# Block ends of a two-layer graph network on one core: transposes by part of the identity in two steps, quotients between two adds, the output's last part in two

## The chip, the cores and the metric

One Trainium2 chip, one NeuronCore. The metric is the device time of one execution in microseconds (us); times shown are medians of several runs. The profile is of one further execution.

## The reference

A graph with 3327 nodes of 128 features and a 0/1 adjacency matrix goes through two layers. Layer 0 is a mean aggregation with batch normalisation; layer 1 is attention in which the adjacency matrix is added (twice) to the scores. `q`, `k` and `v` are reshaped as (128, 3327, 8), so there are 128 attention problems, here called batches, with head size 8. Cut to what matters:

```python
h = relu(layernorm(x))
agg = adj.T @ h / deg
y = agg @ W_n.T + b_n + h @ W_c.T + b_c
x = x + relu(batchnorm(y))                       # layer 0
h = relu(layernorm(x))
q, k, v = ((h @ W.T).reshape(128, n, 8) for W in (Wq, Wk, Wv))
a = einsum('dnh,dmh->dnm', q, k) * 128**-0.5 + adj + adj
out = einsum('dnm,dmh->dnh', softmax(a, axis=2), v)
x = x + out.reshape(n, 1024) @ Wo.T              # layer 1
```

## The kernel before

The order of instructions on each engine is the order in which the program writes them; no scheduler moves them, and semaphores are set from the tiles that instructions share.

**Layer 0** takes some 250 us. At its end the new `x` (`xs`, 26 chunks of 128 rows) is stored to the DRAM tensor `xd` by `keep_nodes`: the first two quarters of four chunks from `residual`, the other 18 chunks at the end on SP's DMA queue. The normalised, transposed activations are stored to `hd` by `keep_columns` on POOL's queue. Then POOL and ACT copy the first set of keys into place, and attention starts.

**Attention** works in `NG` = 32 groups of four batches. A group goes through seven query blocks of 476 columns (`QB`; the last has 472), a block through `SU` = 13 steps, 2912 steps in all. The keys lie in 26 chunks of 128; a step handles four pairs of (key chunk, half of the batches). For each pair `product` (L742) makes the scores of two batches, 128 x 952, in one of three pairs of PSUM banks (`psc`). There are two ways from scores to weights:

- *Plain pairs*: VectorE adds the adjacency to the scores (`add`, L852), and one ACT exponential per step (`late`, L895, issued a step later) handles the two or three plain tiles `d`.
- *Weighted pairs*: ACT takes the exponential of the raw scores (`weighted`, L861), and POOL multiplies it by an exponential of the adjacency read from the DRAM tensor `wd` (L864).

Ten steps have three plain pairs and one weighted; the steps in `DOUBLE` = (3, 7, 11) have two of each. Three steps later (`LAG`) `second(0)` and `second(1)` multiply the weights with `v` (`weigh`, L618) and sum over the chunks in PSUM tile `av`: nine rows for each of four batches, at partitions 0, 32, 64 and 96; the ninth row is the sum of weights. `av` has two buffers, used in turn by the blocks.

**A block's end** is the generator `finish`, driven one part at a time by `step()` in the steps of `PARTS`, at the end of the step between its last product and `second(1)`. With the lag these are steps of the next block. Before, the parts are: at step 3 the copy of `av` to `avs` (L628); at step 5 four transposes of it (L633), each of every fourth column (`J` = 4, so 119 columns, or 118 after the last block), against the whole identity; at step 7 the quotients (L640 to L643: clip, reciprocal, product) on VectorE; at step 8 the store of the result to `att`.

**Side work** uses the `av` bank that a block's end has just left free. `begin`, called after `second(1)`, starts a part at step 7 or 11 (`DOUBLE[1:]`), `go_on` carries it on. In blocks 0 to 2 of a group these are the six halves of the projections of later rows (`projection`, L208, then a VectorE copy `pf` or `ov`, L214 to L236, and stores); in blocks 3 and 4 the output of the rows before (`outputs`): two sets of four transposes (`turn`, L269), then `last`, eight accumulated matmuls with `Wo` (L277) and the addition of `xj` (L282), with the store to `out`.

In group 0 the weights `wd` of the first query columns are there, and `more_weights` makes those of each next block: it loads two chunks of the adjacency (`t`, SP's queue), takes their exponential on ACT (L770), and stores them to `wd`, one pair of chunks in each three steps. Also in group 0, `others` holds 16 loads of the first group's `q` beyond column 512; SP issues two in each step from step 0. SP's queue also carries the fetches of adjacency (`at`, L730) and weights (`wt`, L726), two steps ahead (`PRE`).

The lines around the change in a step:

```python
add(0, product(i, y, *plain[0]))
second(0)
add(1, product(i, y, *plain[1]))
if len(rest) > 1:
    weighted(rest[1][0], product(i, y, *rest[1]))
else:
    add(2, product(i, y, *plain[2]))
if s in PARTS:
    step()
if s - 1 in DOUBLE and x + 1 < len(steps):
    coming = first(x + 1)
second(1)
begin(i, y, s)
go_on(i, y, s)
```

Of the kernel before, what the change touches and what calls it, by code (L numbers as in the profile page):

```python
# [9 lines left out]
F32 = mybir.dt.float32  # L10
# [9 lines left out]
D = 128  # L20
H = 8
P = 128
NC = 26
T = N * D
NP = NC * P
NB = 512
QB = 476
G = 4
# [4 lines left out]
WC = 18  # L33
CH = 4 * NP // D
NG = D // G
DOUBLE = (3, 7, 11)
PARTS = (3, 5, 7, 8)

def pieces(r):

    return [(p0, p1) for p0, p1 in ((0, r // 16 * 16), (r // 16 * 16, r)) if p1 > p0]
# [3 lines left out]
def tile_two_layer_gnn(  # L47
# [17 lines left out]
    nc = tc.nc  # L65
# [6 lines left out]
    qblocks = [(n0, min(QB, NP - n0)) for n0 in range(0, NP, QB)]  # L72
# [16 lines left out]
    wd = dram.tile([NC - WC, P, NP], F32, name="wd")  # L89
    xd = dram.tile([NP, D], F32, name="xd")  # L90
# [163 lines left out]
    def outputs(wk, j):  # L254

        r = min(CH, N - j * CH)
        t = wk.tile([P, H, D], F32, name="t4")
        nc.sync.dma_start(
            t[:CH].rearrange("p e j -> p (e j)"), atr[j * CH : (j + 1) * CH, :]
        )  # L260
        xj = wk.tile([P, D], F32, name="xj")
        nc.sync.dma_start(xj[:CH], xd[j * CH : (j + 1) * CH, :])
        tT = wk.tile([P, H, P], F32, name="t4")

        def turn(e):
            bank = yield
            pt = bank.rearrange("p (i q) -> p i q", i=4)
            for i in range(4):
                nc.tensor.transpose(pt[:, i, :CH], t[:CH, 4 * e + i, :], ident[:CH, :CH])  # L269
            yield  # L270
            nc.vector.tensor_copy(tT[:, 4 * e : 4 * e + 4, :CH], pt[:, :, :CH])
            yield

        def last():
            bank = yield
            for e in range(H):
                nc.tensor.matmul(  # L277
                    bank[:CH, :D], tT[:, e, :CH], wo[:, e, :], start=(e == 0), stop=(e == H - 1)
                )
            yield  # L280
            y = wk.tile([P, D], F32, name="y")
            nc.vector.tensor_add(y[:CH], bank[:CH, :D], xj[:CH])  # L282
            yield
            for p0, p1 in pieces(r):
                nc.sync.dma_start(out[j * CH + p0 : j * CH + p1, :], y[p0:p1])

        return [turn(0), turn(1), last()]

    def drive(part, bank=None):

# [7 lines left out]
    with tc.tile_pool(name="l0", bufs=1) as l0, tc.tile_pool(  # L298
        name="l0adj", bufs=3
# [42 lines left out]
        def stats(i, root=True):  # L342
            cs = range(4 * i, min(NC, 4 * i + 4))
            for c in cs:
                nc.vector.bn_stats(st[:, c, :], xs[:, c, :])
            for c in cs:
                nc.vector.bn_aggr(mv[:, c, :], st[:, c, :])
            if root:
                roots(4 * i, min(NC, 4 * i + 4))

        def roots(c0, c1):
            nc.scalar.activation(sd[:, c0:c1], mv[:, c0:c1, 1], AF.Sqrt, bias=eps)
# [176 lines left out]
        def keep_nodes(cs):  # L529
            nc.sync.dma_start(  # L530
                xd.rearrange("(c p) d -> p c d", p=P)[:, cs, :], xs[:, cs, :]
            )

        def residual(i):
            pt, cs = turned(i, A, acc[i])
            nc.vector.tensor_add(xs[:, cs, :], xs[:, cs, :], pt)
            if i < 2:
                keep_nodes(cs)

        def second_norm(i, engine):  # L540
# [14 lines left out]
        def keep_columns(i0, i1):  # L555
            s = slice(4 * i0 * P, min(NC, 4 * i1) * P)
            nc.gpsimd.dma_start(hd[:, s], B2[:, s])
# [37 lines left out]
        for i in range(2, NQ):  # L595
            if i > 2:
                residual(i)
            stats(i, False)
        roots(4, NC)
        factors(4, NC)  # L600
        for i in range(1, NQ):
            second_norm(i, nc.gpsimd if i % 3 == 0 else nc.vector)
        for i in range(1, NQ):
            columns(i, i % 2 == 0)
        keep_nodes(slice(8, NC))
        keep_columns(0, NQ)
        for x, c in enumerate(range(0, NC, 4)):
            n = min(4, NC - c)
            (nc.scalar.copy if x % 2 else nc.gpsimd.tensor_copy)(
                k[:, c : c + n, :],  # L610
                ks.bitcast(F32).rearrange("g (p c) -> g c p", c=NC)[:, c : c + n, :],
            )

# [7 lines left out]
    def finish(rp, av, d0, n0, w):  # L623

        J = 4
        R = -(-w // J)
        avs = rp.tile([P, QB], F32, name="avs")
        nc.vector.tensor_copy(avs[:, : R * J], av[:, : R * J])  # L628
        yield

        pt = av.rearrange("p (j q) -> p j q", j=J)
        for j in range(J):
            nc.tensor.transpose(  # L633
                pt[:R, j, :], avs[:, j : j + (R - 1) * J + 1 : J], ident
            )
        yield
        pv = pt.rearrange("p j (b h) -> p b j h", h=32)
        ri = rp.tile([P, G, J], F32, name="ri")

        nc.vector.tensor_scalar(ri[:R], pv[:R, :, :, H], 1e-30, None, ALU.max)  # L640
        nc.vector.reciprocal(ri[:R], ri[:R])  # L641
        o = rp.tile([P, G, J, H], F32, name="oq")
        nc.vector.tensor_tensor(  # L643
            o[:R], pv[:R, :, :, :H], ri[:R].unsqueeze(3).to_broadcast([R, G, J, H]),
            ALU.mult,
        )
        yield

        r, j = divmod(min(w, N - n0), J)
        nc.sync.dma_start(  # L650
            attb[bass.ds(d0, G), n0 : n0 + r * J, :].rearrange(
                "b (p j) h -> p b (j h)", j=J
            ),
            o[:r].rearrange("p b j h -> p b (j h)"),
        )
        if j:
            nc.sync.dma_start(
                attb[bass.ds(d0, G), n0 + r * J : n0 + r * J + j, :].rearrange(
                    "b (o j) h -> o b (j h)", o=1
                ),  # L660
                o[r : r + 1, :, :j, :].rearrange("p b j h -> p b (j h)"),
            )
# [4 lines left out]
    def attention():  # L667


        with tc.tile_pool(name="adj", bufs=4) as ap, tc.tile_pool(  # L670
# [13 lines left out]
            if True:  # L684
# [69 lines left out]

                def more_weights(i, y, s):

                    k, phase = s // 3, s % 3
                    if i or y + 1 >= len(qblocks) or k > 3:
                        return
                    n0, w = qblocks[y + 1]  # L760
                    c = WC + 2 * k
                    n = min(2, NC - c)
                    if phase == 0:
                        have["w"] = wk.tile([P, 2, QB], F32, name="t4")
                        nc.sync.dma_start(
                            have["w"][:, :n, :w], adjr[:, c : c + n, n0 : n0 + w]
                        )
                    elif phase == 1:
                        a = have["w"][:, :n, :w]
                        nc.scalar.activation(a, a, AF.Exp, bias=low, scale=2.0)  # L770
                    else:
                        nc.sync.dma_start(
                            wd[c - WC : c - WC + n, :, n0 : n0 + w].rearrange("c p n -> p c n"),
                            have["w"][:, :n, :w],
                        )

# [51 lines left out]
                for x, (i, y, s) in enumerate(steps):  # L830
# [7 lines left out]
                    while pending and (total - len(pending)) * (SU * len(qblocks) - FROM[i] - 4) <= k * total:  # L838
                        pending.pop(0)()
                    more_weights(i, y, s)  # L840
                    for args in others[:2]:
                        nc.sync.dma_start(*args)
                    del others[:2]
                    due = len(waiting) == LAG
                    plain, rest = pairs(s)
                    d = ep.tile([P, 3, 2, QB], F32, name="d")
# [2 lines left out]
                    def add(j, p):  # L849
                        c = plain[j][0]  # L850

                        nc.vector.scalar_tensor_tensor(  # L852
                            d[:, j, :, :w],
                            have[0, i, y, c // 2][:, c % 2, :w]
                            .unsqueeze(1).to_broadcast([P, 2, w]),
                            SAFE / 2, p[:, :, :w], ALU.min, ALU.add,
                        )
# [18 lines left out]
                        late()  # L876
                    add(0, product(i, y, *plain[0]))
                    second(0)
                    add(1, product(i, y, *plain[1]))
                    if len(rest) > 1:  # L880
                        weighted(rest[1][0], product(i, y, *rest[1]))
                    else:
                        add(2, product(i, y, *plain[2]))
                    if s in PARTS:
                        step()

                    if s - 1 in DOUBLE and x + 1 < len(steps):
# [15 lines left out]
                    step()  # L903
                while ending:
                    step()
                for p, b in zip(outputs(wk, NG - 1), (0, 1, 0)):
                    drive(p, avs2[b])
                    drive(p)
                    drive(p)
# [73 lines left out]
    def general():  # L983
# [65 lines left out]
        with tc.tile_pool(name="gw2", bufs=2) as wk, tc.tile_pool(  # L1049
            name="gp2", bufs=1, space=PSUM  # L1050
        ) as gp:
            banks = [gp.tile([P, NB], F32, name=f"h{i}") for i in range(3)]
            for j in range(NG):
                for p, b in zip(outputs(wk, j), banks):
                    drive(p, b)
                    drive(p)
                    drive(p)
# [47 lines left out]
```

## Time and profile before

| | us |
|---|---|
| median of 3 runs | 10390.24 |
| lowest, highest | 10385.12, 10391.82 |
| profiled execution, its own time | 10385.98 |
| its span, first to last instruction | 10384.2 |
| busy: TensorE (PE) | 9816.7 |
| busy: weight loads (PEld, beside PE) | 2888.6 |
| busy: VectorE (DVE) | 9331.0 |
| busy: ScalarE (ACT) | 9925.5 |
| busy: GpSimd (POOL) | 8443.5 |

Busy times overlap, so they are compared with the span one by one. Matmuls are pipelined, and the ends that the profile gives them are modelled; a busy PE is not a PE at its peak. A group row gives line, engine, operation, output<-inputs, shapes and count, then busy us and the mean ns of one, then the idle time before them and what ended it. A row of the timeline gives start and duration in us and, in brackets, the engine's idle time just before and who ended it. `PEld s L742 <- DVE d L852` in the waits means that the weight load of line 742 had to wait for the VectorE instruction of line 852.

### The profile page before, as it was taken

How to read it: one execution, taken by the hardware profiler on the slowest of the kernel's cores; microseconds unless marked ns; L12 is line 12 of the kernel's file. 1: busy time of each engine (PE TensorE's matmuls, PEld its weight loads, DVE VectorE, ACT ScalarE, POOL GpSimd, SP SyncE). 2: the span in 40 equal slices, each digit the busy share in tenths (PEclk: the TensorE clock that was granted, in tenths of full speed). 3: DMA queues.
4: the chain of work that ended last, by engine and by line, in shares of the span. 5: the costliest groups of instructions: out<-in, count | busy, mean ns of one | idle time of the engine just before them, and what ended most of it. 6: DMA issues, size and time to landing. Idle time of an engine off the chain costs nothing.

```text
span 10384.2 us, 188013 instructions
## 1 busy us (share of the span) xinstructions
PE 9816.7 (95%) x72431; PEld 2888.6 (28%) x72431; DVE 9331.0 (90%) x9501; ACT 9925.5 (96%) x6655; POOL 8443.5 (81%) x4316
## 2 busy tenths in 40 slices
PE   7899999999999999999999999999999999999998
PEld 3222222222222222222222222222222222222222
DVE  5689999999999999999999999999999999999998
ACT  4789999999999999999999999999999999999998
POOL 1678888888888888888888888888888888888887
PEclk9899999999999999999999999999999999999999
DMA  6765666665666665666655666655666555666554
GB/s 232 205 178 161 164 168 167 168 165 158 168 167 168 167 162 161 168 169 168 167 159 163 168 169 167 164 165 159 171 168 167 162 164 164 169 168 165 159 153 129
DMA packets 1115994, 1735.87 MB, mean 167 GB/s; under 512 B 194606, under 2 KB 1091756, under 8 KB 1107404
## 3 DMA queue, kind: packets, MB, share of 16 engines
q1 hardware_dynamic: 1110558, 1717.86, 60.2%
q8 instruction: 568, 9.31, 0.4%
q10 hardware_dynamic: 4350, 4.20, 0.1%
q14 instruction: 342, 2.80, 0.1%
q0 software_dynamic: 176, 1.71, 0.0%
HBM read 1621.05 MB, written 102.38 MB: 166 GB/s over the span
## 4 chain that ended last, share of the span: by engine, by line
POOL 21%; PE 16%; ACT 8%; issue 5%; DVE 3%; DMA 0%; POOLq 0%; ACTq 0%; SPq 0%; DVEq 0%
POOL f L864 20%; PE av L618 8%; PE s L742 6%; ACT f L861 5%; ACT d L895 3%; DVE d L852 2%; PE av L633 1%; POOL k L192 1%; PE av L208 1%; PE av L277 0%; POOL o L238 0%; POOL o L237 0%; DVE oq L643 0%; DVE ri L641 0%; DVE avs L628 0%
## 5 line engine op out<-in xcount | busy, mean ns | idle before, releaser
L864 POOL TENSOR_TENSOR f<-f,wt 128x952 f32<-128x952 f32 (+1 forms) x3584 | 7944.8, 2235 | 1680.6 <-ACT f L861 1660.7
L852 DVE SCALAR_TENSOR_TENSOR d<-at,s 128x952 f32<-128x952 f32 x8064 | 8754.4, 1140 | 606.2 <-PE s L742 447.7
L895 ACT ACTIVATE d<-d 128x2856 f32<-128x2856 f32 (+1 forms) x2912 | 7055.5, 2423 | 12.5 <-DVE d L852 2.3
L618 PE MATMUL av<-d,v 128*9 128x476 f32 x32256 | 5072.3, 567 | 1.9 <-ACT d L895 1.9
L742 PE MATMUL s<-q,k 32*128 32x476 f32 x23296 | 4108.3, 476 | 407.9 <-ACT f L861 334.1
L861 ACT ACTIVATE f<-s 128x952 f32<-128x952 f32 (+1 forms) x3584 | 3436.4, 980 | 224.7 <-PE s L742 220.9
L742 PEld LDWEIGHTS s<-q,k 32*128 32x128 f32 x23296 | 1772.8, 182 | 5631.8 <-DVE d L852 3296.9
L618 PE MATMUL av<-f,v 128*9 128x476 f32 x14336 | 2853.4, 566 | 0.0
L618 PEld LDWEIGHTS av<-d,v 128*9 128x9 f32 x32256 | 583.6, 88 | 1162.3 <-issue 1131.8
L618 PEld LDWEIGHTS av<-f,v 128*9 128x9 f32 x14336 | 316.6, 88 | 153.1 <-issue 139.6
L192 POOL CAST k<-ks 128x256 fp32r<-128x256 f32 x434 | 284.6, 656 | 0.0
L633 PE MATMUL av<-ident,avs 128*119 128x128 f32 (+1 forms) x896 | 241.3, 392 | 0.8 <-DVE avs L628 0.8
L633 PEld LDWEIGHTS av<-ident,avs 128*119 128x119 f32 (+1 forms) x896 | 198.2, 292 | 52.7 <-issue 51.1
L430 PE MATMUL acc<-a,A 128*128 128x512 f32 (+1 forms) x364 | 151.8, 570 | 23.2 <-ACT A L364 23.1
L238 POOL TENSOR_TENSOR o<-pf,o 104x512 fp32r<-104x512 f32 x124 | 159.9, 1289 | 9.9
L628 DVE COPY avs<-av 128x476 f32<-128x476 f32 (+1 forms) x224 | 144.6, 645 | 4.5 <-PE av L618 4.5
L437 DVE TENSOR_REDUCE amax<-a 128x1 f32<-128x3327 f32 x26 | 93.7, 3611 | 35.3 <-DMA a<-in_adj 35.3
L236 DVE TENSOR_SCALAR pf<-av,low_half 104x512 f32<-104x512 f32 x62 | 46.6, 751 | 72.0 <-PE av L208 70.3
L234 DVE COPY pf<-av 104x512 f32<-104x512 f32 x62 | 42.9, 692 | 73.0 <-PE av L208 71.8
L214 DVE COPY ov<-av 104x512 f32<-104x512 f32 x62 | 42.9, 692 | 67.8 <-PE av L208 67.8
L430 PEld LDWEIGHTS acc<-a,A 128*128 128x128 f32 x364 | 69.0, 192 | 108.3 <-issue 84.7
L770 ACT ACTIVATE t<-t,low_half 128x952 f32<-128x952 f32 (+1 forms) x24 | 26.2, 1090 | 65.4 <-DMA t<-in_adjT 65.4
(121 smaller groups left out, 1022.6 us busy)
## 6 DMA issues: line engine op xcount, KB each, us to landing
at<-in_adjT SPq DMA_DIRECT2D x1728, 476.0 KB
wt<-wd SPq DMA_DIRECT2D x1536, 238.0 KB
at<-in_adjT SPq DMA_DIRECT2D x288, 472.0 KB
wt<-wd SPq DMA_DIRECT2D x256, 236.0 KB
ks<-kT SPq DMA_DIRECT2D x496, 104.0 KB
q<-qT SPq DMA_DIRECT2D x496, 104.0 KB
a<-in_adj SPq DMA_DIRECT2D x26, 1663.5 KB
kT<-o SPq DMA_DIRECT2D x128, 208.0 KB
```

The source lines that it names most:

```text
L192: nc.gpsimd.tensor_copy(k[:, c : c + n, half * 64 : half * 64 + 64], ks.bitcast(F32).rearrange("g (p c) -> g c p", c=NC)[:, c : c + n, :],)
L208: nc.tensor.matmul(bank[:CH], hj, wqk[s][:, e * NB : (e + 1) * NB], start=True, stop=True)
L238: nc.gpsimd.tensor_tensor(o[:CH, 1], f[:CH], o[:CH, 0].bitcast(F32), ALU.subtract)
L430: nc.tensor.matmul(acc[i][:, :w], A[:, c, :], a[:, n0 : n0 + w], start=(c == 0), stop=(c == NC - 1),)
L618: nc.tensor.matmul(av[32 * b : 32 * b + H + 1, :w], tiles[2][:, b, c, :], e, start=first, stop=last,)
L628: nc.vector.tensor_copy(avs[:, : R * J], av[:, : R * J])
L633: nc.tensor.transpose(pt[:R, j, :], avs[:, j : j + (R - 1) * J + 1 : J], ident)
L742: nc.tensor.matmul(p[:, x, :we], k[rs, c, :], q[rs, n0 : n0 + we], start=True, stop=True,)
L852: nc.vector.scalar_tensor_tensor(d[:, j, :, :w], have[0, i, y, c // 2][:, c % 2, :w] .unsqueeze(1).to_broadcast([P, 2, w]), SAFE / 2, p[:, ...
L861: nc.scalar.activation(f[:, :, :w], p[:, :, :w], AF.Exp, scale=2.0)
L864: nc.gpsimd.tensor_tensor(f[:, :, :w], f[:, :, :w], have[1, i, y, c][:, :w].unsqueeze(1).to_broadcast([P, 2, w]), ALU.mult,)
L895: nc.scalar.activation(flat, flat, AF.Exp, scale=2.0)
```

## The change

A block's end gets one part more, at step 6: the four transposes become plain matmuls of `avs` with 36 columns of the identity (nine for each batch), two at step 5 and two at step 6, and the results lie densely in the bank. At step 7 `step()` moves from after the step's last product to between its first and second plain add. `last` is split into two parts of four matmuls, the second adding to the sum of the first, so the output has four parts of side work. In layer 0 the third quarter of `xs` is stored from `residual` too, the other 14 chunks on POOL's queue ahead of the second normalisation, and the store to `hd` comes after the copies of the keys. In group 0 `more_weights` takes the exponential two steps after the load, and the store comes three after it, just ahead of the next load; the loads in `others` start at step 2. The path `general`, which this input does not take, gets a fourth bank.

```diff
-PARTS = (3, 5, 7, 8)
+PARTS = (3, 5, 6, 7, 8)
...
-        def last():
+        y = wk.tile([P, D], F32, name="y")
+
+        def last(i):
             bank = yield
-            for e in range(H):
+            for e in range(4 * i, 4 * i + 4):
                 nc.tensor.matmul(
-                    bank[:CH, :D], tT[:, e, :CH], wo[:, e, :], start=(e == 0), stop=(e == H - 1)
+                    bank[:CH, :D], tT[:, e, :CH], wo[:, e, :],
+                    start=(e == 4 * i), stop=(e == 4 * i + 3),
                 )
             yield
-            y = wk.tile([P, D], F32, name="y")
-            nc.vector.tensor_add(y[:CH], bank[:CH, :D], xj[:CH])
+            nc.vector.tensor_add(y[:CH], bank[:CH, :D], y[:CH] if i else xj[:CH])
             yield
-            for p0, p1 in pieces(r):
-                nc.sync.dma_start(out[j * CH + p0 : j * CH + p1, :], y[p0:p1])
+            if i:
+                for p0, p1 in pieces(r):
+                    nc.sync.dma_start(out[j * CH + p0 : j * CH + p1, :], y[p0:p1])
...
-        return [turn(0), turn(1), last()]
+        return [turn(0), turn(1), last(0), last(1)]
...
-            if i < 2:
+            if i < 3:
                 keep_nodes(cs)
...
+        nc.gpsimd.dma_start(
+            xd.rearrange("(c p) d -> p c d", p=P)[:, 12:, :], xs[:, 12:, :]
+        )
         roots(4, NC)
...
-        keep_nodes(slice(8, NC))
-        keep_columns(0, NQ)
         for x, c in enumerate(range(0, NC, 4)):
...
+        keep_columns(0, NQ)
...
-        pt = av.rearrange("p (j q) -> p j q", j=J)
+        pt = av[:, : J * G * (H + 1)].rearrange("p (j q) -> p j q", j=J)
+        some = ident.rearrange("p (b h) -> p b h", h=32)[:, :, : H + 1]
         for j in range(J):
-            nc.tensor.transpose(
-                pt[:R, j, :], avs[:, j : j + (R - 1) * J + 1 : J], ident
-            )
-        yield
+            nc.tensor.matmul(
+                pt[:R, j, :], avs[:, j : j + (R - 1) * J + 1 : J], some, start=True, stop=True
+            )
+            if j % 2:
+                yield
...
-                    k, phase = s // 3, s % 3
-                    if i or y + 1 >= len(qblocks) or k > 3:
+                    k, phase = divmod(s, 3)
+                    if i or y + 1 >= len(qblocks):
                         return
...
+                    if phase == 0 and k:
+                        nc.sync.dma_start(
+                            wd[c - 2 - WC : c - WC, :, n0 : n0 + w].rearrange("c p n -> p c n"),
+                            have["w"][:, :, :w],
+                        )
+                    if c == NC:
+                        return
...
-                    elif phase == 1:
-                        a = have["w"][:, :n, :w]
+                    elif phase == 2:
+                        a = have["w"][:, :, :w]
                         nc.scalar.activation(a, a, AF.Exp, bias=low, scale=2.0)
-                    else:
-                        nc.sync.dma_start(
...
-                    for args in others[:2]:
-                        nc.sync.dma_start(*args)
-                    del others[:2]
+                    if x > 1:
+                        for args in others[:2]:
+                            nc.sync.dma_start(*args)
+                        del others[:2]
...
                     second(0)
+                    if s == DOUBLE[1]:
+                        step()
                     add(1, product(i, y, *plain[1]))
...
-                    if s in PARTS:
+                    if s in PARTS and s != DOUBLE[1]:
                         step()
```

More of the change, by code (lines that the diff above doesn't have):

```diff
@@ L629, in finish @@
         yield
-        pt = av.rearrange("p (j q) -> p j q", j=J)
+        pt = av[:, : J * G * (H + 1)].rearrange("p (j q) -> p j q", j=J)
+        some = ident.rearrange("p (b h) -> p b h", h=32)[:, :, : H + 1]
         for j in range(J):
-            nc.tensor.transpose(
-                pt[:R, j, :], avs[:, j : j + (R - 1) * J + 1 : J], ident
-            )
-        yield
-        pv = pt.rearrange("p j (b h) -> p b j h", h=32)
+            nc.tensor.matmul(
+                pt[:R, j, :], avs[:, j : j + (R - 1) * J + 1 : J], some, start=True, stop=True
+            )
+            if j % 2:
+                yield
+        pv = pt.rearrange("p j (b h) -> p b j h", h=H + 1)
         ri = rp.tile([P, G, J], F32, name="ri")
@@ L761, in more_weights @@
                     c = WC + 2 * k
-                    n = min(2, NC - c)
+                    if phase == 0 and k:
[5 more added lines that the diff above has]
+                        return
                     if phase == 0:
@@ L765, in more_weights @@
                         nc.sync.dma_start(
-                            have["w"][:, :n, :w], adjr[:, c : c + n, n0 : n0 + w]
+                            have["w"][:, :, :w], adjr[:, c : c + 2, n0 : n0 + w]
                         )
-                    elif phase == 1:
-                        a = have["w"][:, :n, :w]
+                    elif phase == 2:
+                        a = have["w"][:, :, :w]
                         nc.scalar.activation(a, a, AF.Exp, bias=low, scale=2.0)
-                    else:
-                        nc.sync.dma_start(
-                            wd[c - WC : c - WC + n, :, n0 : n0 + w].rearrange("c p n -> p c n"),
-                            have["w"][:, :n, :w],
-                        )
                 extra, begun = [], []
@@ L905, in attention @@
                     step()
-                for p, b in zip(outputs(wk, NG - 1), (0, 1, 0)):
+                for p, b in zip(outputs(wk, NG - 1), (0, 1, 0, 1)):
                     drive(p, avs2[b])
@@ L1051, in general @@
         ) as gp:
-            banks = [gp.tile([P, NB], F32, name=f"h{i}") for i in range(3)]
+            banks = [gp.tile([P, NB], F32, name=f"h{i}") for i in range(4)]
             for j in range(NG):
```

## The prediction

> **What bounds the kernel now.** I read the page first, then busy times by block, then the waits, then the timeline around one block's end, then the groups kept apart by shape. The page's first line:
>
> ```profile
> PE 9816.7 (95%) x72431; PEld 2888.6 (28%) x72431; DVE 9331.0 (90%) x9501; ACT 9925.5 (96%) x6655; POOL 8443.5 (81%) x4316
> ```
>
> ScalarE (ACT) is the fullest. The stretches between block ends show which blocks leave it idle. Below are five of the seven of group 15: from the end of its second block on, each row is start:end, length, then busy time of PE, PEld, DVE, ACT, POOL.
>
> ```profile
> 5104.37:5149.28 44.91, 43.51 (x322) 12.36 (x322) 41.43 (x43) 43.78 (x30) 39.47 (x22) 1.00 0.66 185
> ...
> 5194.16:5238.49 44.33, 42.49 (x326) 12.62 (x326) 41.41 (x44) 43.65 (x30) 36.44 (x19) 1.00 0.60 160
> 5238.49:5284.05 45.56, 43.60 (x332) 13.97 (x332) 40.62 (x42) 43.56 (x30) 35.98 (x18) 1.00 0.59 159
> 5284.05:5328.16 44.11, 41.39 (x320) 11.98 (x316) 40.39 (x42) 43.44 (x30) 37.85 (x21) 1.00 0.60 149
> 5328.16:5372.24 44.08, 41.35 (x320) 11.89 (x316) 40.27 (x41) 43.38 (x30) 36.38 (x19) 1.00 0.52 156
> ```
>
> ACT's busy time is nearly constant (43.4 to 43.8), the length is not. A block with no side work takes 44.1; one with two projection halves 44.9; one with the output's `last` 45.56. The step itself is ACT's: in the timeline its `d` exponentials start 3.32 us apart in a plain step and 4.16 in a double one, without a gap. So only what makes ACT idle counts. Waits by who waited for whom:
>
> ```profile
> PEld av L208 <- DVE oq L643: 134.0, 92, 1.5
> ...
> ACT t L770 <- DMA t<-in_adjT: 65.4, 13, 10.1
> ...
> PEld av L269 <- DVE oq L643: 45.2, 31, 1.5
> ```
>
> ACT waits outright for the loads of more_weights; TensorE waits for the quotients with side work in hand. Third, the end of a block in the timeline (start, duration):
>
> ```profile
> 5021.15 0.19 PEld L742 LDWEIGHTS s<-q,k 32*128 32x128 f32 x4 [0.79 <-DVE d L852]
> ...
> 5021.57 0.94 PEld L633 LDWEIGHTS av<-ident,avs 128*119 128x119 f32 x4 [0.23 <-issue]
> ...
> 5022.64 0.10 PEld L618 LDWEIGHTS av<-d,v 128*9 128x9 f32 x3
> ...
> 5024.12 0.96 ACT L861 ACTIVATE f<-s 128x944 f32<-128x944 f32 x1 [0.70 <-PE s L742]
> ```
>
> The four transposes hold TensorE 1.07 us (5021.57 to 5022.64), and ACT's next `f` finds no scores for 0.70. So this place forgives 0.37. Why: of three score banks the step's last product takes the one that `f` frees; from there product, transposes, four weighted products and the next first product run in series while ACT does one `d`. The block with 118 columns agrees: transposes 0.64, idle 0.27. In block length the price is a little more than the idle, since an `f` that follows idle time loses its overlap with the `d` before: the step with 1.07 is 0.84 longer, that with 0.64 is 0.52.
>
> **What the Trainium skill says.** "TensorE: Matmul & The Clock Gate", section LDWEIGHTS (loading the stationary operand): a load costs its columns / 1.2 ns, whatever the depth. The weight loads by shape:
>
> ```profile
> L618 PEld LDWEIGHTS av<-d,v 128*9 128x9 f32 x32256 | 583.6, 88 | 1162.3 <-issue 1131.8 <-ACT d L895 3.7 <-ACT t L770 0.2
> ...
> L633 PEld LDWEIGHTS av<-ident,avs 128*119 128x119 f32 x768 | 181.5, 309 | 44.0 <-issue 44.0
> ...
> L277 PEld LDWEIGHTS av<-wo,t 128*104 128x104 f32 x512 | 58.3, 173 | 45.6 <-DVE oq L643 45.3 <-DVE t L271 0.3
> ...
> L633 PEld LDWEIGHTS av<-ident,avs 128*118 128x118 f32 x128 | 16.7, 195 | 8.7 <-issue 7.1 <-DVE avs L628 1.6
> ```
>
> Nine to 104 columns: (173 - 88) / 95 = 0.9 ns a column, which agrees. The transposes with 119 don't: (309 - 88) / 110 = 2.0. "FP8 and Floating Point Precision", TensorE Precision Notes: true FP32 is four passes; the trace agrees, each fp32 matmul stands as two instructions (46,592 at L618 for eight calls in each of 2,912 steps), a transpose as one. "SBUF — State Buffer", Specifications (TRN2): full bandwidth wants two hits in each 16-byte line. The slices of avs step four floats, 16 bytes, so each column is a new line. Whether that slows a plain fp32 load no instruction before shows; it is the large unknown.
>
> **The change, part by part.** Sums are made against the profiled execution, 10,386.0 us (span 10,384.2), 4 below the median 10,390.2.
>
> *1. Quotients between two adds (step 7).* Before, they sit behind step 7's last add (5029.60 to 5030.37, 0.79 with gaps), and TensorE's side work, next in its queue, waits: its load stands 1.47 after the last against 0.80 unhindered, 0.67 lost. A projection half then holds TensorE 1.04 (L208 at 5119.09, products at 5120.12), and ACT idles 0.35. For `last`, 1.92 and 1.24. Both give the same forgiveness, 0.67 + 1.04 - 0.35 = 1.36 and 0.67 + 1.92 - 1.24 = 1.35: more than before, since a double step has a second `f` here. Now the quotients start some 1.1 earlier, ahead of TensorE's need; 1.04 alone is under 1.35, as step 11 shows, where the same 1.04 meets no quotients and costs nothing. Prices by block: 0.7 three times (projections), 0.14 (output transposes), 1.55 (`last`), 3.8 a group. I leave 0.7, as DVE's copy `pf` (0.75) still stands between adds there: 3.1 x 31 groups = **96 us saved**, `last` in two included. The halves of `last` are 8 instructions, 1.05, at steps 7 and 11. It adds 32 adds of 0.29 on DVE (9 us in all, in blocks where DVE is busy 40.6 of 45.6); without that cover, +9.
> The price of the move: the second add of step 7 comes 0.79 later. Behind it stand the next step's first add and, through the bank it frees, TensorE's second product of step 8. The add after those starts at 5032.26, after 0.73 of waiting for a product, so the delay ends there; `d` of step 7 starts at 5032.40, two us after its add would now end. Nothing, or at worst 0.79 x 224 = 177.
>
> *2. The transposes.* Four transposes of one instruction become four matmuls of two, with 36 columns moving for 128, half of them at step 5, half at step 6. A half is four weight loads of 119. At 0.86 ns a column, 0.10 each, plus 0.13 for the last matmul and turnaround (the tail of the output's last, 0.31, less 0.10 for the load and 0.08 for 92 columns fewer): 0.53. Over 0.37 it leaves 0.16 idle; with the lost overlap 0.36. Fourteen halves a group cost 5.0, where now six blocks at 0.84 and one at 0.52 cost 5.5: 0.5 x 32 = **17 us saved**. Bounds: if a half fits, all 178 goes; if a load keeps the 2.0 ns of this tile (0.22 each), a half is 1.01, costs 0.78 (0.23 less than its length, as 1.07 costs 0.84), 10.9 a group: +173. I take the plain rate because nine odd columns load at it, and since L633's matmuls with 119 are slower than those with 118 too (408 ns against 300 in the same view), though their moving operand is the same: the oddness of the transpose slows both, without the step in memory.
>
> *3. more_weights.* Load, exponential one step later, store two later; now the exponential two later and the store three. ACT takes its instructions in order, so a late load holds it. The 13 waits are 10.1, 1.3, 4.0, 5.6, 5.8, 5.7, 0.8, 3.8, 5.5, 6.0, 6.3, 7.9 and 2.6; a plain step of 3.3 off each leaves 27.7: **38 saved**. The 24 exponentials stay (1.09 each). SP's store waits for the exponential, and behind it the pair's next load and the fetches; the exponential precedes the `f` whose POOL product already paces SP. Bounds 20 to 55.
>
> *4. Stores and loads at layer 0's end.* SP issues a third xd store (0.4) ahead of the kT and qT stores, and is rid of the large one ahead of the first adjacency fetch; POOL issues 14 chunks before its second norm, where it waits for ACT anyway (to 242.28), then the k copies before the hd store (0.6). The late q loads start two steps later and end at step 9; the next block needs them at 13. DMA is 97% busy from 250 to 300, so order matters more than issue: xd now competes with the k loads, hd with the first fetches. I take 5 saved, -8 to +12. In the tail, one more short add: under 1.
>
> Sum: -96 - 17 - 38 - 5 = -156, that is 10,230, and 10,234 by the median. I say **10,240**, as part 1 is nearer its upper bound than the others.
>
> **Rivals.**
> *The strided load stays slow (ends slower).* Place: steps 5 and 6 of every block. Price +173 against -139 for the rest: 10,390 + 34 = 10,424. It decides where fourteen halves cost 5.5 + 139 / 32 = 9.8, that is 0.70 each: a half of 0.93 us, 0.20 for each load. For it: every column on a new line, and the 309 ns above. Against it: the 195 of 118 columns at the same step.
> *The quotients hold DVE (slower).* Against it, the slack named; +177 - 156: 10,411.
> *DVE is the bound in side-work blocks.* It is busy 41.4 of 44.9 there; then part 1 gives 15 or so: 10,315.
> *The halves fit.* 178 instead of 17: 10,073.
> That the change doesn't do what it says I don't count: the instruction order has all of it.
>
> **The numbers.** Likeliest case 0.58 (own range 10,180 to 10,300), slow load 0.23 (with loads between the two prices), quotients 0.06, DVE 0.08, fit 0.05. A measurement tells 0.2%, 21 us, from no change. Faster: 0.57 + 0.08 + 0.05 + 0.02 = 0.72; same 0.01 + 0.08 + 0.02 = 0.11; slower 0.13 + 0.04 = 0.17. The range takes in the slow load's 10,424 and leaves out the full fit: 10,170 to 10,425.
>
> **What would show it.** Right: the new transposes' halves under 0.6 with two idle spells of some 0.15 each before `f`; no L208 load waiting for oq; blocks with projections within 0.3 of those without; ACT's wait for t under 30. Wrong: weight loads of 119 at about 300 ns and idle of 0.6 at steps 5 and 6; a DVE wait of ACT's `d` in step 7 or 8; a `last` block still 1 us long.

## The result and the profile after

| | before | after |
|---|---|---|
| median of 20 runs each, us | 10384.39 | 10376.67 |
| profiled execution, span, us | 10384.2 | 10380.2 |

The ratio is 0.9991, with a 95% interval of 0.9985 to 0.9997: 8 us faster where 150 were forecast. That is inside the 0.2% which the prediction set as no change. (The median before is 6 us lower here than in the prediction, as it is of more runs.) So nearly the whole expected gain is missing, and the profile after shows that it did arrive, in one place, and was spent in another.

The page's first line: ScalarE's (ACT) busy time has hardly moved, TensorE's (PE) and its weight loads' (PEld) have grown by 179 and 194 us.

```profile
PE 9995.3 (96%) x73327; PEld 3082.3 (30%) x73327; DVE 9366.9 (90%) x9533; ACT 9923.2 (96%) x6655; POOL 8439.0 (81%) x4317
```

The same five stretches between block ends of group 15 as before (start:end, length, then busy time of PE, PEld, DVE, ACT, POOL):

```profile
5089.50:5134.24 44.74, 44.02 (x326) 13.18 (x326) 41.52 (x43) 43.66 (x30) 39.45 (x22) 1.00 0.68 188
...
5179.00:5223.73 44.73, 43.16 (x330) 13.42 (x330) 41.69 (x43) 43.66 (x30) 36.42 (x19) 1.00 0.64 159
5223.73:5268.66 44.93, 44.18 (x338) 14.42 (x338) 40.87 (x43) 43.80 (x30) 36.16 (x18) 1.00 0.59 161
5268.66:5313.09 44.43, 42.82 (x320) 13.07 (x320) 40.47 (x41) 43.36 (x30) 37.65 (x21) 1.00 0.60 149
5313.09:5357.69 44.60, 42.78 (x324) 12.97 (x320) 40.35 (x41) 43.50 (x30) 36.33 (x19) 1.00 0.53 154
```

The blocks have become more alike. The one with `last` fell from 45.56 to 44.93 (44.8 in most groups), the projections' from 44.91 to 44.74: side work is nearly free. But the blocks without side work, where little was to be gained, rose from 44.11 and 44.08 to 44.43 and 44.60, and so did the one with the output's transposes, from 44.33 to 44.73. Over the seven blocks of a group the two cancel: 312.6 us before, 313.1 after.

The waits after show what went (total us, times, longest):

```profile
PEld av L208 <- DVE oq L651: 72.6, 91, 0.8
...
PEld av L269 <- DVE oq L651: 24.7, 31, 0.8
...
ACT t L784 <- DMA t<-in_adjT: 9.7, 5, 3.3
```

The longest wait of a projection for the quotients is 0.8 instead of 1.5, which is what a load in that place shows without any wait; ACT's wait for the loaded adjacency is 10 us instead of 65. What came in its place is ACT's waits for scores, first of before, then of after:

```profile
ACT f L861 <- PE s L742: 220.9, 343, 3.8
```

```profile
ACT f L871 <- PE s L750: 266.0, 426, 8.9
```

They take 45 us more, against 56 less for the adjacency, so ACT waits in all about as long as before. The block's end in the timeline after, weight loads and ACT's `f` at steps 5 and 6 (start, duration; this block's end has 118 columns):

```profile
5050.56 0.94 PEld L640 LDWEIGHTS av<-ident,avs 128*118 128x118 f32 x4 [0.23 <-issue]
5051.54 0.10 PEld L623 LDWEIGHTS av<-d,v 128*9 128x9 f32 x3
...
5053.04 0.97 ACT L871 ACTIVATE f<-s 128x952 f32<-128x952 f32 x1 [0.60 <-PE s L750]
...
5054.47 0.94 PEld L640 LDWEIGHTS av<-ident,avs 128*118 128x118 f32 x4 [0.23 <-issue]
5055.45 0.12 PEld L623 LDWEIGHTS av<-f,v 128*9 128x9 f32 x8
...
5056.96 0.97 ACT L871 ACTIVATE f<-s 128x952 f32<-128x952 f32 x1 [0.47 <-PE s L750]
```

Each half holds TensorE for 0.98 us (5050.56 to 5051.54), almost as long as the whole did before (1.07), and ACT idles twice, 0.60 and 0.47, where it idled once, 0.70. The reason stands in the weight loads by shape (after the bar the busy us, then the mean ns of one load):

```profile
L640 PEld LDWEIGHTS av<-ident,avs 128*119 128x119 f32 x1536 | 363.0, 309 | 87.3 <-issue 87.3
...
L640 PEld LDWEIGHTS av<-ident,avs 128*118 128x118 f32 x256 | 59.9, 307 | 15.8 <-issue 14.2 <-DVE avs L633 1.6
```

A plain fp32 load of these columns takes 309 ns, and with an even count 307. The slow rate was not left behind with the transposes: now every block has eight such loads instead of four, and the 118 columns, which loaded in 195 ns as a transpose, are slow too.

### The profile page after: what moved, and what is told of

Its sections match the earlier page's. It is cut to its first block, busy times and chain, and to the rows that moved or that the text cites. A ratio compares the mean times of both kernels' runs of the same rounds, so it can differ in the third digit from the quotient of the medians.

```text
span 10380.2 us, 189900 instructions
## 1 busy us (share of the span) xinstructions
PE 9995.3 (96%) x73327; PEld 3082.3 (30%) x73327; DVE 9366.9 (90%) x9533; ACT 9923.2 (96%) x6655; POOL 8439.0 (81%) x4317
## 5 line engine op out<-in xcount | busy, mean ns | idle before, releaser
L871 ACT ACTIVATE f<-s 128x952 f32<-128x952 f32 (+1 forms) x3584 | 3396.9, 970 | 281.8 <-PE s L750 266.0
L750 PEld LDWEIGHTS s<-q,k 32*128 32x128 f32 x23296 | 1739.5, 182 | 5500.2 <-DVE d L862 3005.9
L640 PE MATMUL av<-ident,avs 128*119 128x36 f32 (+1 forms) x1792 | 474.1, 391 | 0.8 <-DVE avs L633 0.8
L640 PEld LDWEIGHTS av<-ident,avs 128*119 128x119 f32 (+1 forms) x1792 | 422.9, 308 | 103.1 <-issue 101.5
L406 POOL TENSOR_TENSOR sq<-wk 128x512 f32<-128x512 f32 x2 | 2.1, 1042 | 102.5 <-PE aside L407 102.5
L437 ACT ACTIVATE junk<-a 128x3327 bf16<-128x3327 f32 x26 | 77.5, 2979 | 7.1 <-DMA a<-in_adj 6.8
```

Of the source, the lines that this page charges most:

```text
L640: nc.tensor.matmul(pt[:R, j, :], avs[:, j : j + (R - 1) * J + 1 : J], some, start=True, stop=True)
L750: nc.tensor.matmul(p[:, x, :we], k[rs, c, :], q[rs, n0 : n0 + we], start=True, stop=True,)
L871: nc.scalar.activation(f[:, :, :w], p[:, :, :w], AF.Exp, scale=2.0)
```

## The experiments

The theory after the comparison: four parts that add, of which the transposes take what the others give, through the 16-byte step of the loaded columns. Rivals: that 119 columns are slow as a plain matmul in any layout; that the odd count is what makes them slow; that VectorE, not TensorE, holds the side work.

**The transposes alone.** The kernel before with

```diff
-PARTS = (3, 5, 7, 8)
+PARTS = (3, 5, 6, 7, 8)
...
-            nc.tensor.transpose(pt[:R, j, :], avs[:, j : j + (R - 1) * J + 1 : J], ident)
+            nc.tensor.matmul(pt[:R, j, :], avs[:, j : j + (R - 1) * J + 1 : J], some, ...)
+            if j % 2:
+                yield
```

> The kernel before with the new transposes alone (plain matmuls with 36 columns, half at step 5, half at step 6). Theory: each half holds TensorE 0.99 us because a weight load whose columns lie 16 bytes apart takes twice as long; a block loses 0.77 + 0.60 at steps 5 and 6 where it lost 0.84 (0.52 with 118 columns): 0.53 x 6 + 0.85 = 4.0 a group, +129 us over 32 groups, ratio 1.012. Rival: the halves cost no more than the whole did, and the gain was lost elsewhere: ratio 0.998.

Measured: 10542.03 us against 10386.79, ratio 1.0148 (1.0132 to 1.0163), +155 us. The idle at steps 5 and 6 is that of the changed kernel (0.60 and 0.47). The part above +129 is not in the theory: in this kernel, where the quotients still stand late, ACT's idle in step 7 beside a projection is 0.51 instead of 0.35. In the trace each of the five blocks with side work takes 0.15 longer around that step; by 5 blocks and 31 groups that is 23 us.

**The quotients and the output alone.** The kernel before with `step()` between the first and second add at step 7, and `last` in two parts.

> The kernel before with the quotients between two adds at step 7 and the output's last part in two, nothing else. Theory: the side work in blocks 0 to 4 becomes nearly free, 3.8 a group less some 0.2: -112 us, ratio 0.989, and no L208 load waits longer than 0.8 us. Rival: VectorE is the bound in these blocks, and little comes back: -15 us, ratio 0.9985. Second rival: the add that now stands behind the quotients delays every block by up to 0.79: +60 us and more.

Measured: 10281.43 us, ratio 0.9896 (0.9881 to 0.9911), -105 us. Its waits have the 0.8 of the changed kernel:

```profile
PEld av L208 <- DVE oq L646: 73.4, 92, 0.8
```

ACT's idle in step 7 is gone in every block; only the 0.68 of the transposes at step 5 is left. VectorE is not the bound there, and the add behind the quotients delays nothing. What the quotients gave and what the halved `last` gave was not tried apart.

**The later exponential alone.** In `more_weights` of the kernel before:

```diff
-                    elif phase == 1:
+                    elif phase == 2:
                         nc.scalar.activation(a, a, AF.Exp, bias=low, scale=2.0)
```

with the store moved ahead of the next pair's load.

> The kernel before with the later exponential and store in more_weights alone. Theory: ACT's wait for the loaded adjacency falls from 65 to under 15 us, but in group 0 other waits take up part of it (for scores, behind a TensorE clock that is below full there): -25 us, ratio 0.9976. Rival: all of it comes back: -50 us, 0.995. Other rival: nothing, as DMA is the bound in group 0.

Measured: 10359.44 us, ratio 0.9972 (0.9961 to 0.9983), -27 us. Its waits:

```profile
ACT f L862 <- PE s L742: 241.3, 357, 6.2
...
ACT t L776 <- DMA t<-in_adjT: 17.5, 10, 4.7
```

ACT's wait for `t` is 17.5 us instead of 65.4, so 48 us of waiting made 27 of time. The rest stands in the first row: ACT waits 20 us longer for scores than before (241.3 against 220.9). That the TensorE clock is the reason for those waits was not tried.

**The stores at layer 0's end alone.** `xd`'s third quarter from `residual`, the rest from POOL ahead of the second normalisation, `hd` after the key copies, the late `q` loads from step 2.

> The kernel before with the moved stores of xd and hd and the later q loads alone. Theory: it costs time. The first exponential of scores starts 5.8 us later since the k loads share the DMA engines with the store of xd, and the first add waits until the store of hd, issued later, has been read out of the memory that the first d tile takes over: +6 to +9 us, ratio 1.0007. Rival: a gain of 5 us, as forecast, 0.9995.

Measured: 10390.82 us, ratio 1.0003 (0.9994 to 1.0011): not told from no change. The timeline shows where the start differs, first of before, then of this kernel (VectorE's first adds, and the wait ahead of them):

```profile
262.79 6.43 DVE L852 SCALAR_TENSOR_TENSOR d<-at,s 128x952 f32<-128x952 f32 x6 [13.38 <-DMA wt<-wd]
```

```profile
270.64 10.65 DVE L855 SCALAR_TENSOR_TENSOR d<-at,s 128x952 f32<-128x952 f32 x10 [17.68 <-DMA hd<-B]
```

The first add is 8 us later, and the profile names the store of `hd` as what it waits for. That the first `d` lies on memory which that store still reads is the likely reason; it was not tried. ACT's first `d` is only 2.8 us later (273.93 against 271.13), as before it came behind a wait for `t` that ended at 269.29; the first block end is 3.5 later (344.6 against 341.1 us).

**Consecutive columns in the changed kernel.**

```diff
-        nc.vector.tensor_copy(avs[:, : R * J], av[:, : R * J])
+        nc.vector.tensor_copy(
+            avs[:, : R * J].rearrange("p (j r) -> p r j", j=J),
+            av[:, : R * J].rearrange("p (r j) -> p r j", j=J),
+        )
...
-                pt[:R, j, :], avs[:, j : j + (R - 1) * J + 1 : J], some, ...
+                pt[:R, j, :], avs[:, j * R : (j + 1) * R], some, ...
```

> The changed kernel, but VectorE writes the copy avs with the columns of each transpose side by side, so that the weight loads read consecutive floats. Theory (the 16-byte step is what makes a load slow): the loads of 119 start 0.10 us apart instead of 0.22, a half takes 0.53 instead of 0.99, ACT idles 0.15 instead of 0.60 and 0.47 per block, 4.6 us a group less: -147 us against the changed kernel, ratio to before 0.985. Rival (119 columns of a plain fp32 matmul are slow in any layout): ratio 0.999 as before. What the permuted write of the copy costs VectorE comes on top in both.

Measured: 10175.86 us against 10385.48, ratio 0.98 (0.9783 to 0.9816), some 200 us below the changed kernel by their ratios. Its loads:

```profile
L643 PEld LDWEIGHTS av<-ident,avs 128*119 128x119 f32 x1536 | 189.6, 183 | 87.1 <-issue 87.1
...
L643 PEld LDWEIGHTS av<-ident,avs 128*118 128x118 f32 x256 | 31.1, 181 | 16.1 <-issue 14.2 <-DVE avs L633 1.9
```

183 ns instead of 309: the same instruction, the same 119 columns, only side by side. One half in the timeline:

```profile
4905.55 0.49 PEld L643 LDWEIGHTS av<-ident,avs 128*119 128x119 f32 x4 [0.23 <-issue]
4906.08 0.10 PEld L623 LDWEIGHTS av<-d,v 128*9 128x9 f32 x3
```

The loads start 0.10 us apart, a half takes 0.53, and ACT idles 0.16 at step 5 and 0.02 at step 6. In the trace the two steps are 0.31 and 0.14 longer than an undisturbed one, where the expectation reckoned with 0.36 for each half; that is why more came back than 147. This is the run that decides the theory against the first rival.

**Consecutive columns with the old transposes.** The kernel before, with the same permuted copy.

> The kernel before with the same permuted copy: its four transposes read 119 consecutive columns. If the odd count alone makes a transpose slow, nothing changes: loads 0.22 us apart, ratio 1.000. If the step is what matters, they come down to about 0.11, the whole from 1.07 to 0.62 us: 0.4 x 6 x 32 = -77 us, ratio 0.9926.

Measured: 10303.24 us, ratio 0.9923 (0.9906 to 0.9939), -82 us.

```profile
L636 PEld LDWEIGHTS av<-ident,avs 128*119 128x119 f32 x768 | 97.0, 183 | 43.8 <-issue 43.8
...
L636 PEld LDWEIGHTS av<-ident,avs 128*118 128x118 f32 x128 | 13.2, 136 | 9.0 <-issue 7.1 <-DVE avs L628 1.9
```

An odd count alone costs a transpose something, 183 against 136 ns, and so does the step alone: the 118 columns of before took 195. The 309 of before needs both. TensorE is held 0.63 us by four odd transposes without the step, 0.64 by four even ones with it, and 1.07 by odd ones with it.

**120 columns.** As the run just before this one, with a garbage column more so that the count is even.

> As the kernel before last, but each transpose takes 120 columns (a garbage row more, which is not stored), even and consecutive. Either theory: fast loads, the four transposes in about 0.6 us, a block at 0.45 instead of 0.84 at step 5: -75 us, ratio 0.9928. Beside the run with 119 it tells the odd count from the step.

Measured: 10290.55 us, ratio 0.9909 (0.9893 to 0.9926); the intervals of the last two runs overlap. The loads take 138 ns, and the idle at step 5 is 0.19 against 0.24.

**The block's end in a double step.** Copy between two adds at step 3, all transposes (120 consecutive columns) at its end, quotients at step 5.

> The kernel before with the block's end moved instead of split: the copy (permuted, 120 columns) between two adds at step 3, all four transposes at the end of step 3, a double step, the quotients at step 5, the store at step 6; the output's last part in two and the later more_weights as in the change, the stores of layer 0 as before. Theory: a double step forgives 1.35 us, so 0.6 of transposes cost nothing even if TensorE waits up to 0.5 for the copy, and the quotients are long done at step 7: -178 - 105 - 27 = -310 us, ratio 0.970. Rival: TensorE waits for the copy longer than that, and step 3 idles: up to 0.7 a block, +150 on top, 0.985.

Measured: 10295.85 us, ratio 0.9913 (0.9896 to 0.993), -90 instead of -310: a miss, by more than the rival. TensorE does wait for the copy:

```profile
PEld av L639 <- DVE avs L631: 269.1, 221, 1.9
...
ACT f L868 <- PE s L748: 87.1, 173, 5.7
```

The `d` exponentials in the timeline show two losses. The double step around the transposes is 0.54 longer. And in the plain step with the quotients, which have three adds ahead of them there, the next `d` comes late:

```profile
5012.78 0.95 ACT L868 ACTIVATE f<-s 128x952 f32<-128x952 f32 x1
5014.01 2.59 ACT L904 ACTIVATE d<-d 128x2856 f32<-128x2856 f32 x1 [0.27 <-DVE d L859]
```

From `d` to `d` this step takes 3.70 (5010.31 to 5014.01) instead of 3.32. Together 0.92 a block, 206 us, about what is missing. So the quotients seem to need their place between two adds of a double step; that place was not tried alone.

**Two and two.** Quotients, output and `more_weights` as in the change, layer 0 as before, four true transposes of 120 consecutive columns, two each at steps 5 and 6:

```diff
+        R = -(-w // (2 * J)) * 2
...
+            nc.tensor.transpose(pt[:R, j, :], avs[:, j * R : (j + 1) * R], ident)
+            if j % 2:
+                yield
```

> Quotients, output and more_weights as in the change, the stores of layer 0 as before, and the block's end as four true transposes of 120 consecutive columns, two at step 5 and two at step 6 (permuted copy at step 3). Theory: two transposes take 0.06 us to the second load and some 0.35 to the next weighted product, 0.40 together, so ACT hardly idles; a block costs 0.2 to 0.3 where the plain matmuls on consecutive columns cost 0.49: 40 to 60 us below that kernel, and 5 more for layer 0: ratio to before 0.974. Rival: the remaining cost is VectorE's (the permuted copy of 1.04 us), not TensorE's: no faster than plain matmuls, 0.980.

Measured: 10103.83 us, ratio 0.9729 (0.9716 to 0.9743). A half in the timeline, and its loads:

```profile
4968.09 0.20 PEld L639 LDWEIGHTS av<-ident,avs 128*120 128x120 f32 x2 [0.22 <-issue]
4968.46 0.10 PEld L621 LDWEIGHTS av<-d,v 128*9 128x9 f32 x3 [0.17 <-issue]
```

```profile
L639 PEld LDWEIGHTS av<-ident,avs 128*120 128x120 f32 x768 | 74.8, 138 | 87.3 <-issue 87.3
```

A half holds TensorE for 0.37 us (4968.09 to 4968.46), just the 0.37 that step 5 forgives, and ACT's idle at steps 5 and 6 is gone in every block. Step 5 still takes 3.46 from `d` to `d` instead of 3.32 in the mean over the trace; by 224 blocks that is 31 us. The plain matmuls on consecutive columns with layer 0 as here (the next run) take 65 us more; the kind of instruction and the even count changed together between the two, so what each gave is not told. Its page:

```profile
PE 9753.2 (96%) x72431; PEld 2772.5 (27%) x72431; DVE 9358.7 (93%) x9533; ACT 9892.4 (98%) x6655; POOL 8433.7 (83%) x4316
```

**Consecutive columns without the stores' move.** The changed kernel with the permuted copy, layer 0 as before.

> The changed kernel with consecutive columns, and the stores and q loads of layer 0's end as before. Theory: the moved stores cost 5 to 10 us at the start of attention (first block end at 331 us instead of 340): ratio to before 0.979, against 0.980 with them. Rival: they gain 5: 0.9805. A difference under 0.1% will not be told by the times, but the start of the first add shows it in the trace.

Measured: 10169.04 us, ratio 0.9793 (0.978 to 0.9806), against 0.98 with the moved stores; the times don't tell them apart. In the trace the first add starts at 264.3 us without the move and at 267.9 with it.

**The step on the other side of the copy.** As the two-and-two kernel, the copy reading in steps and writing consecutively.

> As the kernel with 120 consecutive columns in two halves, but the copy reads av in steps and writes avs consecutively. Theory: VectorE's time for the copy depends on which side has the step: under 1.0 us; the time of the kernel changes by less than 0.2% either way, since VectorE has slack at step 3. Rival: VectorE's time counts, and 0.3 us a block is 70 us.

Measured: 10101.68 us, ratio 0.973 (0.9715 to 0.9745), the same as two and two. The copy takes 651 ns instead of 1047, and the times don't show it: VectorE has slack at step 3. These two are the fastest versions found: 2.7% below the kernel before.

## Why the prediction was wrong

**Part 2 is the step that failed**, at "I take the plain rate". What was wrong was the rate of a load in the layout that the change has: 309 ns a load and 0.98 us a half, the 2.0 ns a column of the other bound, where the prediction had 0.10 us from load to load and 0.53 a half. The signs that it had named for this came out: loads of about 300 ns, and idle of 0.60 and 0.47 at steps 5 and 6. The sum built on the rate was sound: once the columns were consecutive, the loads stood 0.10 us apart and a half took 0.53.

The first argument for the plain rate was that nine odd columns load at it; those lie side by side, so they said nothing on the step. The second laid the slow transposes to their odd count "without the step in memory". But an odd transpose with consecutive columns loads in 183 ns and an even one with the step in 195, so their 309 came of both together; and a plain load has the slow rate with an even count too (307). The same table held a warning: the 118 columns at 195 ns, which I read as fast, are slow for an even transpose (136 when consecutive).

The price of a half was wrong too, the other way. The prediction let every plain step forgive 0.37 us, from what it saw at step 5. Step 5 did so, within 0.01 (0.98 held and 0.60 idle after the change, 0.53 and 0.16 with consecutive columns). Step 6 forgave 0.51 in both kernels (0.98 and 0.47, 0.53 and 0.02). Why it forgives more was not settled.

The Trainium skill had a line that fits: "SBUF — State Buffer", Specifications (TRN2), wants two hits in each 16-byte line for full bandwidth. The prediction cited it, noted that each column is a new line, and then chose against it. The runs agree with the page: over twice the time a column for plain loads (with the 88 ns of nine columns taken off, 221 against 95 ns over 110 columns). They do not tell the 16-byte line from a step as such, as none has a step of two or three floats. The four passes that the prediction cites for true FP32 are not shown: the trace has two instructions for each fp32 matmul (46,592 at L618), and the sums use only those.

The rival "the strided load stays slow" is what happened. It priced two halves at 0.78 each; they cost 0.77 and 0.60 in step time, 7 x 1.37 = 9.6 a group against 5.5, so the part is some +130 and not +173. That is near the 132 us that parts 1 and 3 gave alone, so the sum ended at almost no change instead of 34 us slower; that they balance so closely is chance.

**Part 1 was right.** Forecast -96, measured alone -105 (interval -124 to -92). The idle in step 7 went altogether, so the 0.7 a group left for VectorE's copy was too careful; the prices themselves were a little high, as 105 us is 3.4 a group and not 3.8. The forgiveness of 1.35 us in a double step held for work in place; what it did not cover, in the kernel with everything at step 3, was a wait for a copy of 1.0 us ahead of it.

**Part 3 was right in kind:** -27 for -38, inside its bounds of 20 to 55; the interval, -40 to -18, does not tell the two apart. By the traces ACT's wait for the loads fell by more than forecast, 48 us, and waits for scores, which the prediction left out, took 20 of it back.

**Part 4's sign is not shown.** Forecast -5, measured +4 with an interval of -6 to +11 us. What the prediction did not name is that the first add then waits for the `hd` store: VectorE idles 17.7 us ahead of it instead of 13.4.

**The sum.** +155 - 105 - 27 + 4 is +27, where the change measured -8. Of these 35 us, 23 are the extra time around step 7 that the transposes cause only while the quotients are late; the rest is within the intervals of the four comparisons. In the spans of the two profiles, group 0 with its start and the tail gave 18 us, and groups 1 to 31 took 14 back, 0.45 each.

Of the other rivals, the quotients did not hold VectorE, VectorE is not the bound in blocks with side work, and the halves fit, by ACT's idle, only in the kernels with true transposes of 120 consecutive columns: the first took 10,104 us, 31 above the 10,073 of that rival, about what step 5 still loses there.

## What to carry to other kernels

When a matmul's stationary operand is a slice with a step, look up what one load of it takes before counting columns: here consecutive columns were worth 200 us in a kernel of 10,400, for a changed access pattern in one copy. An operation that stands in a fixed chain between two uses of a buffer has a forgiveness that can be read from two of its sizes, for each place by itself (0.37 us at step 5 here, 0.51 at step 6); fitted under that, it cost little, 0.14 us of step time. And don't carry a rate over from another instruction unless layout, count and kind agree: here each of the three made a difference somewhere.

## What the runs showed of the hardware

Weight loads of fp32, mean duration by layout: plain, 119 columns consecutive 183 ns, with a step of 16 bytes 309; transposes, 118 or 120 consecutive 136 to 138, 119 consecutive 183, 118 with the step 195, 119 with the step 309. So the step counts for both kinds, and the odd count for transposes alone; for these the two together cost more (173 ns) than each by itself added up (59 and 47). VectorE's copy of 128 x 476 from PSUM takes 646 ns straight, 651 when it reads PSUM in steps of four floats (480 columns), and 1042 when it writes SBUF in steps of 119 floats instead.
